# Splitting five of the seven half-wide products of the aggregates a second time (two-layer graph attention network, fp32)

## The chip, the cores and the metric

The kernel runs on one core of one Trainium2 chip. The metric is the device time of one execution in microseconds (us); a figure for a kernel is the median of several executions. The profile is one further execution, recorded by the hardware profiler.

## What is computed

Two layers of graph attention over N = 2708 rows of width D = 1024, all fp32. `adj` (2708 x 2708, int32) says which pairs of rows are joined.

```python
h = relu(layernorm(x))                      # layer 0
f, g = h @ Wf + bf, h @ Wg + bg
e = relu(f @ g.T)
a = softmax(where(adj > 0, e, -9e15), axis=1)
x = x + a @ (h @ W + bW)

h = relu(layernorm(x))                      # layer 1
hW = h @ W1
e = leaky_relu(hW @ a1 + (hW @ a2).T)
a = softmax(where(adj > 0, e, -9e15), axis=1)
x = x + relu(a @ hW)
```

Both kernels reorder this: `a @ (h @ W)` is taken as `(a @ h) @ W`, and `f @ g.T` as `h @ (Wf Wg^T) @ h.T` with the biases added as vectors. The score matrix is kept transposed: attended rows lie on partitions, attending rows in columns.

## The kernel before, in words

*Tiling.* The 2708 attending rows are cut into five column panels of 576, 576, 532, 512 and 512 (`width`). The attended rows are 20 tiles of 128, in ten pairs (`NQ` = 10), and a rest of 128 + 20 rows (`MONO` and `TINY`, the left-over tiles). The width of 1024 is two halves of `W` = 512, and each half four chunks of 128 (`NH` = 4).

*One level of Strassen.* Every large product is a 2 x 2 block product in the form that Winograd gave to Strassen's method: seven products of half-size blocks (`M1` to `M7`) in place of eight, with sums and differences of blocks before and after. In an aggregate the left blocks are halves of two paired row tiles, the right blocks the two halves, `lo` and `hi`, of a panel's columns. A half-wide product of panel p therefore streams h = `width[p]`/2 columns: 288, 288, 266, 256 and 256. Operations on the operands and the joins of the results run on VectorE (DVE in the profile); its additions and subtractions all have line L45, since a helper issues them.

*The stages of layer 0.* First M = Wf Wg^T. Then for each panel:

- `project_q` (L639) makes the right side of the scores, M times the panel's rows; in it `hT` (L643) holds the turned rows of the panel, in the two large buffers of pool `gts` that the aggregates' results `gT` use too.
- `scores` (L1115) goes through the ten pairs; each takes seven products of four matmuls (L1140) with the operands `As`, 512 KB a load, adds the biases, applies relu and the mask, and keeps the column maximum. Masks are made from `adj` a pair ahead.
- `softmax` subtracts the maximum, exponentiates on ScalarE and sums.
- `aggregate` (L841) multiplies the weights with the rows: `accumulate` (L603) takes the products in the order M1, M5, M2, M6, M3, M7, M4, each of 10 pairs x 4 chunks = 40 matmuls (L617) into four PSUM banks. The left operands `hc` are 512 KB loads of two pairs of one of seven prepared forms of the rows (`hg_d`, in DRAM). `left_over` (L877, matmuls on L883 and L887) adds the rest of 128 + 20 rows. `second` and `fourth` (L857, L864) make the differences of the weights that the later products need. `scale` (L931) divides by the sums on POOL.
- `project` (L965) multiplies the result with W, whose blocks `w` are loaded by `load_W` (L955), in matmuls of 512 columns (L1029); `finish0` (L1348) adds the residual and the bias and hands the finished rows to `rows_done` (L1283), which prepares layer 1: layernorm, the prepared forms of the rows (`pair_h`, L309), dot products and maxima.

Layer 1 has no scores matrix product. `weights1` (L1460) makes the weights from two vectors; then follow `aggregate` and `project` per panel.

*Order.* TensorE works through its list in program order. All loads are issued by SP in program order (L139), all stores by POOL (L143). Between the matmuls the helper `behind(rate)` (L198) works off a list of tasks, `later`, which `put` fills: each task may have a load that is issued a few tasks ahead. So the layernorm of later rows, the preparation of layer 1, the preparation of W (`prepare_W`, L1067) and the weights of layer 1 run beside the matmuls. Where `nc.hold` names VectorE, its program order is kept as well; elsewhere a scheduler orders it.

The main loop (L1423 to L1457) takes, for the first panels, `scores(p)`, `project_q(p+1)`, `aggregate(p)`, `project(p)`; after the first aggregate it empties the task list (`flush`, L1447). For the last two panels the projection comes a stage later: scores 4, projection 3, aggregate 4, projection 4.

*Buffers.* SBUF has 54 buffers of one panel row (`slots`, L118) for weights, sums and temporaries, and 12 of 4 KB per partition (`strm`, L119) through which everything streams that is loaded. PSUM has eight banks of 512 columns.

Of the kernel before, what the change touches and what calls it, by code (L numbers as in the profile page):

```python
# [57 lines left out]
def kernel(  # L58
# [59 lines left out]
    slots = ctx.enter_context(tc.tile_pool(name="slots", bufs=54))  # L118
    strm = ctx.enter_context(tc.tile_pool(name="strm", bufs=12))  # L119
# [34 lines left out]
    groups = [[q, q + 1] for q in range(0, NQ, 2)]  # L154
    group_of = {q: (i, j) for i, g in enumerate(groups) for j, q in enumerate(g)}
    assert sorted(group_of) == list(range(NQ))
    hg_d = [[dram.tile([P, 7, len(g), W], FP, name=f"hg{l}_d{i}") for i, g in enumerate(groups)] for l in range(2)]
    hsl_d = dram.tile([P, 2, NH, P], FP, name="hsl_d")
    hgl_d = [dram.tile([P, 2, W + P], FP, name=f"hgl{l}_d") for l in range(2)]
# [141 lines left out]
    def left_h(l, hm, ht):  # L301

        for e in range(2):
            store(hgl_d[l][:, e, :W], hm[e])
            for d in range(NH):
                g = slice(B32 * d, B32 * (d + 1))
                store(hgl_d[l][g, e, W:], ht[e][g, d * P:(d + 1) * P])

    def pair_h(l, q, ha, hb):  # L309
# [3 lines left out]
        if q >= NQ - F // 2:  # L313
            s1, s2, s3, s4 = (slot(f"g{i}")[:, :W] for i in range(4))
            i, j = group_of[q]
            for m, h in ((M1, ha[0]), (M2, hb[0]), (M4, hb[1])):
                store(hg_d[l][i][:n, m, j], h)
            on.tensor_tensor(s1, ha[1], hb[1], OP.add)
            on.tensor_tensor(s2, s1, ha[0], OP.subtract)
            for m, h in ((M5, s1), (M6, s2)):  # L320
                store(hg_d[l][i][:n, m, j], h)

            def rest():
                on.tensor_tensor(s4, hb[0], s2, OP.subtract)
                on.tensor_tensor(s3, ha[0], ha[1], OP.subtract)
                for m, h in ((M3, s4), (M7, s3)):
                    store(hg_d[l][i][:n, m, j], h)
# [7 lines left out]
        i, j = group_of[q]  # L335
        for m, h in ((M1, ha[0]), (M2, hb[0]), (M4, hb[1])):
            store(hg_d[l][i][:n, m, j], h)
        store(hg_d[l][i][:n, M5:M6 + 1, j], g1[:n])
        store(hg_d[l][i][:n, M7:M3 + 1, j], g2[:n])

    def rows_h(q, ha, hb):

        i, j = group_of[q]
        for m, h in ((M1, ha[0]), (M5, ha[1]), (M2, hb[0]), (M4, hb[1])):
            store(hg_d[0][i][:, m, j], h)
# [3 lines left out]
    def sums_h():  # L349

        def fetch(q, two):
            i, j = group_of[q]
            for m in (M1, M2):
                two.append(stream("hr", (P, 2, W)))
                load(two[-1], hg_d[0][i][:, m:m + 2, j])
# [6 lines left out]
        def second(q, two):  # L362
# [3 lines left out]
            i, j = group_of[q]  # L366
            store(hg_d[0][i][:, M6:M7 + 1, j], two[0])
            store(hg_d[0][i][:, M3, j], b0)
            store(hg_d[0][i][:, M5, j], b1)
            summed[0] += 1  # L370
        for q in range(NQ):
            two = []
            put(1.4, lambda q=q, two=two: first(q, two), lambda q=q, two=two: fetch(q, two))
            put(1.4, lambda q=q, two=two: second(q, two))

# [263 lines left out]
    def project_q(p, then={}):  # L639
# [3 lines left out]
        R = first_h if p == 0 else both("hT")  # L643
        lo, hi = (t.rearrange("p (c i) -> p c i", c=NH) for t in R)
        o = 0
        for t, n in pieces[p]:
            if p == 0:
                break
            for e, side in enumerate((lo, hi)):
                s = side[:, :, o:o + n]  # L650
                if t == TINY:
                    nc.scalar.copy(s, tinyT[:, e, :, :NY])
                elif t == MONO:
                    load(s, hsl_d[:, e, :, NM:])
                else:
                    q, k = pair_of[t]
                    load(s, hs_d[q][:, (BY_SCORES.index(M4 if k else M2) if e else 7 if k else BY_SCORES.index(M1))])
            o += n
        T1 = in_pairs("qT1")
        for g in range(2):  # L660
            sub(T1[g][:, :, :h], lo[:, 2 * g:2 * g + 2, h:w], lo[:, 2 * g:2 * g + 2, :h])
        sub(lo[:, :, h:w], hi[:, :, h:w], lo[:, :, h:w])

        def second():
            for g in range(2):
                sub(lo[:, 2 * g:2 * g + 2, :h], hi[:, 2 * g:2 * g + 2, h:w], T1[g][:, :, :h])

        def fourth():
            sub(hi[:, :, :h], hi[:, :, :h], lo[:, :, :h])
# [18 lines left out]
        def right(m, k):  # L688
            return {M1: lo[:, k, :h], M2: hi[:, k, :h], M3: hi[:, k, h:w], M5: T1[k // 2][:, k % 2, :h],
                    M6: lo[:, k, :h], M7: lo[:, k, h:w], M4: hi[:, k, :h]}[m]  # L690
# [150 lines left out]
    def aggregate(l, p, S, sm, then={}, rate=3.0):  # L841
# [28 lines left out]
        def left(m, q, d):  # L870
            i, j = group_of[q]
            if (m, i) not in hc:
                hc[m, i] = stream("hc", (P, 2, W))
# [706 lines left out]
```

## Time and profile before

| | us |
|---|---|
| median of 3 runs | 3132.52 |
| lowest and highest of them | 3129.16, 3133.04 |
| span of the profiled execution (the page gives no other time of it) | 3135.8 |
| PE (TensorE matmul) busy | 3053.1 |
| PEld (TensorE weight load) busy | 2266.1 |
| DVE (VectorE) busy | 1835.6 |
| ACT (ScalarE) busy | 450.3 |
| POOL (GpSimd) busy | 427.3 |

All times in the profile are microseconds of that one execution. SP issues the loads. An fp32 matmul appears as two records, each with its own weight load; a row of the profile writes the number of records as x80. The slices of the page cut the span into 40 equal parts, one digit each (9 is 90% or more). A view by stages cuts the span where TensorE's work changes, and gives the busy time of each engine in each stretch, the TensorE clock that was granted (PEclk), the mean busy share of the 16 DMA engines and what they moved. The chain of waits follows the work back from what ended last: each of its rows is a start, a duration, an engine, a tile and a line.

The whole kernel moves 666 MB through the DMA engines, 212 GB/s over the span. The aggregates of layer 0 for panels 1 to 4 take TensorE 148, 137, 132 and 132 us, those of layer 1 150, 138, 134 and 132 us.

### The profile page before, as it was taken

What the parts mean: (1) busy time and instruction counts of PE and PEld (TensorE: products, weight loads), DVE (VectorE), ACT (ScalarE), POOL (GpSimd) and SP (SyncE); (2) the same over time, 40 slices, a digit from 0 to 9 for tenths busy, and PEclk for the clock granted to TensorE, in tenths of its full rate; (3) what the DMA queues carried; (4) which work ended last, traced back from release to release, by engine and by line L of the source; (5) the groups of instructions that cost most, each with busy time, mean ns of one, the idle gap of its engine ahead of it and who ended that gap; (6) DMA issues with size and microseconds to landing.
All of it is one profiled execution on the core that took longest, in us unless ns stands there. A gap on an engine that the chain in (4) does not pass through costs nothing.

```text
span 3135.8 us, 36310 instructions
## 1 busy us (share of the span) xinstructions
PE 3053.1 (97%) x12694; PEld 2266.1 (72%) x12694; DVE 1835.6 (59%) x3767; ACT 450.3 (14%) x785; POOL 427.3 (14%) x654
## 2 busy tenths in 40 slices
PE   8998999899999999999999999998999999999998
PEld 4576777657877588886888885875757758678684
DVE  5766693776741686426973377758573571745612
ACT  3420020010200101101020002103131130311200
POOL 1421101310002110023000101021010020120202
PEclk9999999999999999999999999998999999999999
DMA  6989967988546796468955678597655565565655
GB/s 220 294 252 248 292 247 253 301 275 230 175 136 156 222 247 223 149 153 253 284 180 160 171 214 245 191 293 250 200 179 175 158 200 158 171 197 172 219 169 181
DMA packets 386278, 666.04 MB, mean 212 GB/s; under 512 B 171744, under 2 KB 212224, under 8 KB 386096
## 3 DMA queue, kind: packets, MB, share of 16 engines
q1 hardware_dynamic: 341936, 536.96, 56.9%
q0 software_dynamic: 44160, 126.76, 12.6%
q8 instruction: 101, 1.65, 0.2%
q14 instruction: 81, 0.66, 0.1%
HBM read 548.26 MB, written 115.30 MB: 212 GB/s over the span
## 4 chain that ended last, share of the span: by engine, by line
PE 81%; issue 6%; DVE 6%; DMA 5%; SPq 1%; POOL 1%; ACT 0%; POOLq 0%; DVEq 0%; ACTq 0%
PE gz L617 11%; PE gx L617 11%; PE gy L617 10%; PE sz L1140 6%; PE pz L1029 5%; PE gv L617 5%; PE sx L1140 4%; PE sy L1140 4%; PE px L1029 4%; PE py L1029 4%; PE M_ps L530 3%; PE qz L617 2%; PE qx L617 2%; PE qy L617 2%; DVE junk L45 1%
## 5 line engine op out<-in xcount | busy, mean ns | idle before, releaser
L1140 PE MATMUL sz<-B,As 128*128 128x288 f32 (+2 forms) x1200 | 295.9, 396 | 12.1 <-DVE st L45 7.9
L1140 PEld LDWEIGHTS sz<-B,As 128*128 128x128 f32 x1200 | 229.4, 192 | 63.1 <-DVE st L45 11.8
L933 POOL TENSOR_TENSOR gT<-gT,rr 128x2304 f32<-128x2304 f32 (+5 forms) x20 | 73.0, 3648 | 1081.4 <-DVE rr L45 979.3
L1140 PE MATMUL sx<-B,As 128*128 128x288 f32 (+2 forms) x800 | 201.5, 395 | 11.2 <-DMA As<-hs_d 9.1
L1140 PE MATMUL sy<-B,As 128*128 128x288 f32 (+2 forms) x800 | 199.3, 392 | 0.0
L617 PE MATMUL gz<-Sa,hc 128*128 128x288 f32 (+2 forms) x800 | 190.3, 399 | 5.9 <-DMA hc<-hg_d 5.9
L617 PE MATMUL gx<-P,hc 128*128 128x288 f32 (+2 forms) x800 | 187.0, 394 | 0.1
L617 PE MATMUL gz<-P,hc 128*128 128x288 f32 (+2 forms) x800 | 185.5, 392 | 0.0
L1140 PEld LDWEIGHTS sx<-B,As 128*128 128x128 f32 x800 | 152.5, 191 | 45.2 <-DMA As<-hs_d 10.1
L617 PE MATMUL gy<-T,hc 128*128 128x288 f32 (+2 forms) x800 | 184.2, 391 | 0.0
L617 PEld LDWEIGHTS gz<-Sa,hc 128*128 128x128 f32 x800 | 154.6, 194 | 40.0 <-DMA hc<-hg_d 6.4
L617 PEld LDWEIGHTS gx<-P,hc 128*128 128x128 f32 x800 | 152.4, 191 | 34.2 <-issue 3.7
L1140 PEld LDWEIGHTS sy<-B,As 128*128 128x128 f32 x800 | 152.3, 191 | 30.8
L617 PEld LDWEIGHTS gz<-P,hc 128*128 128x128 f32 x800 | 151.3, 190 | 31.6 <-issue 1.8
L617 PEld LDWEIGHTS gy<-T,hc 128*128 128x128 f32 x800 | 152.0, 190 | 30.5
L1029 PE MATMUL pz<-w,ps 128*128 128x512 f32 x320 | 142.1, 594 | 0.8 <-DVE pt L45 0.8
L1029 PE MATMUL py<-w,ps 128*128 128x512 f32 x320 | 141.9, 593 | 0.0
L1029 PE MATMUL px<-w,gT 128*128 128x512 f32 x320 | 141.0, 593 | 0.0
L143 POOL DMA_DIRECT2D out_dram<-x_res x180 | 89.2, 502 | 269.7 <-DVE x_res L45 264.5
L1029 PEld LDWEIGHTS pz<-w,ps 128*128 128x128 f32 x320 | 60.2, 190 | 77.1 <-issue 71.0
L1029 PEld LDWEIGHTS py<-w,ps 128*128 128x128 f32 x320 | 60.6, 190 | 75.5 <-issue 73.1
L530 PE MATMUL M_ps<-wgT,wfT 128*128 128x512 f32 x256 | 112.9, 597 | 1.6 <-ACT hsT L45 1.6
(319 smaller groups left out, 4894.9 us busy)
## 6 DMA issues: line engine op xcount, KB each, us to landing
hc<-hg_d SPq DMA_DIRECT2D x350, 512.0 KB, 3.7
As<-hs_d SPq DMA_DIRECT2D x150, 512.0 KB, 5.2
w<-wt_d SPq DMA_DIRECT2D x96, 512.0 KB, 4.9
w<-in_L_gnn_W_dram SPq DMA_DIRECT2D x72, 512.0 KB, 4.8
md<-md_d SPq DMA_DIRECT2D x56, 512.0 KB, 5.7
adj_i<-in_adj_dram SPq DMA_DIRECT2D x200, 128.0 KB, 5.2
hs_d<-hsT POOLq DMA_DIRECT2D x40, 512.0 KB, 7.2
As<-hs_d SPq DMA_DIRECT2D x50, 256.0 KB, 4.8
```

Source lines behind the costliest of these rows:

```text
L45: i = f(*a, **k)
L143: nc.gpsimd.dma_start(a, b)
L530: nc.tensor.matmul(ps, wfT[a][c // NH][:, c % NH, :], wgT[b][c], start=(c == 0), stop=(c == NC - 1))
L617: nc.tensor.matmul(ps[d], left(m, k, d), right(m, k), start=(start and k == 0), stop=(k == K - 1), skip_group_check=True)
L933: nc.gpsimd.tensor_tensor(of(e, s), of(e, s), by(s, k), OP.mult)
L1029: nc.tensor.matmul(ps, left[i][m][:, k, :], w_[k], start=(start and k == 0), stop=(k == NH - 1), skip_group_check=True)
L1140: nc.tensor.matmul(ps[:n, :h], lefts[q][:, i % 2, c, :n], B[m][c // 2][:, c % 2, :h], start=(start and c == 0), stop=(c == NH - 1), skip_g ...
```

## The change

**The aggregates of panels 1 to 4, in both layers, become `aggregate_quartered`.** `M1` and `M5` stay as before. The other five (`BY_QUARTERS`, in the order M2, M6, M7, M3, M4) are each split once more: a product of half-size blocks becomes seven products of quarter-size blocks. One such sub-product is five pairs of pairs (`NK` = 5) times two output chunks, ten matmuls with hb = h/2 columns (144, 133, 128, 128), and both output chunks share one PSUM bank.

```diff
+    def aggregate_quartered(l, p, S, sm, then={}, rate=3.0, fine=1.2):
...
+        def quarter_sums(m):
+            for k in range(NK):
+                r11, r12, r21, r22 = (part_of(m, k, i) for i in ((0, 0), (0, 1), (1, 0), (1, 1)))
+                four = slot("quarter", (P, 4, WX // 4))
+                t = {n: four[:, i, :hb] for i, n in enumerate((M5, M6, M7, M4))}
+                sub(t[M5], r12, r11)
+                sub(t[M6], r22, t[M5])
+                sub(t[M7], r22, r12)
+                sub(t[M4], r21, t[M6])
+                sums[m, k] = t
...
+        def product(m, n, ps, start):
+            quarters_until(l, m)
+            t = stream("hc2", (P, NK, WH))
+            if n in (M1, M2, M4):
+                load(t, hr_d[l][:, m, int(n == M4), int(n != M1)])
+            else:
+                load(t, hs2_d[l][:, m, {M5: 0, M6: 1, M7: 2, M3: 3}[n]])
+            for k in range(NK):
+                for d in range(2):
+                    nc.tensor.matmul(ps[:, d], t[:, k, d * P:(d + 1) * P], inner_right(m, n, k),
+                                     start=(start and k == 0 and d == 0), stop=(k == NK - 1), skip_group_check=True)
+            behind(fine)
...
+        before_next = {M2: lambda: (fourth(), quarter_sums(M6)), M6: lambda: quarter_sums(M7),
+                       M7: lambda: quarter_sums(M3), M3: lambda: quarter_sums(M4)}
+        left_out = None
+        for m in BY_QUARTERS:
+            V = in_pairs("V")
...
+            X = bank2("gx")
+            product(m, M1, X, True)
+            nc.scalar.copy(c21, X)
+            if left_out:
+                left_out()
+            Z = bank2("gz")
+            product(m, M6, Z, True)
+            add(c12, Z, c21)
+            Y = bank2("gy")
+            product(m, M5, Y, True)
+            add(c22, Y, c21)
+            if m == M7:
+                corner()
+            if m in before_next:
+                before_next[m]()
+            product(m, M2, X, False)
+            if m not in more_of:
+                nc.scalar.copy(c11, X)
+            product(m, M7, Z, False)
+            add(c22, Z, c22)
+            product(m, M3, Y, False)
+            if m in more_of:
+                U = bank2("gu")
+                left_over({(0, 0): X, (0, 1): Y, (1, 0): Z, (1, 1): U}, *more_of[m], [(1, 1)])
+                nc.scalar.copy(c11, X)
+            add(c12, Y, c12)
+            if m in more_of:
+                add(c22, U, c22)
+            into_place(m, V, 0)
+            def left_out(m=m, V=V, Z=Z, c21=c21):
+                product(m, M4, Z, False)
+                add(c21, Z, c21)
+                into_place(m, V, 1)
...
```

`product` of the last sub-product, M4, follows after the first of the next product (`left_out`). `second` (20 subtractions) and `quarter_sums(M2)` follow in M5; `fourth` writes into the tiles of M5. `scale` stays on POOL. The left-over rows go in by twice as many matmuls of half the columns; the tiny rows in DRAM are stored as two chunks side by side for that (`hgl_d`, W + 128 columns before, W + 256 after).

**The rows' quarter sums.** The seven forms of the rows are stored by quarters (`hr_d`, in place of `hg_d`), and for each of the five products four sums of quarters are made once a layer and stored (`hs2_d`): 25 tasks a layer.

```diff
+    def put_quarters(l, m, k):
+        two = []
+        def fetch():
+            two.append(stream("hq", (P, 4, WH)))
+            load(two[0], hr_d[l][:, m, :, :, k].rearrange("p h f c -> p (h f) c"))
+        def go():
+            a11, a12, a21, a22 = (two[0][:, i] for i in range(4))
+            o = stream("hq2", (P, 4, WH))
+            s1, s2, s3, s4 = (o[:, i] for i in range(4))
+            add(s1, a21, a22)
+            sub(s2, s1, a11)
+            sub(s3, a11, a21)
+            sub(s4, a12, s2)
+            store(hs2_d[l][:, m, :, k], o)
+            made_quarters[l, m] = made_quarters.get((l, m), 0) + 1
+        put(1.7, go, fetch)
+    def quarters_until(l, m):
+        while made_quarters.get((l, m), 0) < NK:
+            one()
```

The 25 tasks of layer 0 are put after the first aggregate, those of layer 1 by `rows_done` when a group of pairs is complete (`quads_met`).

**Order and buffers.** The main loop takes each projection after the next panel's scores; the empty-the-list call after the first aggregate is replaced by `flush_W`, which works off the list after the scores of panel 1 only until W is prepared (`todo_W` counts that).

```diff
-    slots = ctx.enter_context(tc.tile_pool(name="slots", bufs=54))
-    strm = ctx.enter_context(tc.tile_pool(name="strm", bufs=12))
+    slots = ctx.enter_context(tc.tile_pool(name="slots", bufs=53))
+    strm = ctx.enter_context(tc.tile_pool(name="strm", bufs=10))
...
         if p == 0:
...
+            B = project_q(1, hooks)
+            ahead[0] = 1
+            G[0] = aggregate(0, 0, S, got["sm"], {M4: lambda: sums_until(NQ), M5: prepare_W, **masks})
+            ahead[0] = 2
+            for m in BY_QUARTERS:
+                for k in range(NK):
+                    put_quarters(0, m, k)
+            continue
+        if p == 1:
+            flush_W()
+            spread_wa()
+        nc.hold = ("vector",)
+        project(0, p - 1, G.pop(p - 1), finish0(p - 1), hooks)
+        nc.hold = ()
+        if p == NP - 1:
+            scores_before()
+        G[p] = aggregate_quartered(0, p, S, got["sm"])
         if p + 1 < NP:
-            B = project_q(p + 1, hooks)
...
-            flush()
...
+            B = project_q(p + 1, masks)
...
-            then = {M3: lambda p=p: take_shifts(p + 1), M7: lambda p=p: take_weights(p + 1)}
-        g = aggregate(1, p, S, sm, then, rate=4.0)
+            then = dict(zip((M7, M3) if p else (M3, M7), (lambda p=p: take_shifts(p + 1), lambda p=p: take_weights(p + 1))))
+        g = (aggregate_quartered if p else aggregate)(1, p, S, sm, then, rate=4.0)
```

In `project_q`, `hT` no longer uses the two large buffers but four of `strm` (`stream("hT", (P, 2, WX))`), loaded and subtracted in halves of two chunks.

## The prediction

> **What bounds the kernel now.** I read first the busy shares and slices of the page, then the stages (busy time of each engine in stretches cut where the TensorE work changes), then the chain of waits inside one aggregate, then single instructions.
>
> ```profile
> PE 3053.1 (97%) x12694; PEld 2266.1 (72%) x12694; DVE 1835.6 (59%) x3767; ACT 450.3 (14%) x785; POOL 427.3 (14%) x654
> PE   8998999899999999999999999998999999999998
> ```
>
> TensorE is busy in every slice. Of the chain of waits, this is the whole aggregate of layer 0, panel 3:
>
> ```profile
> 1646.00 17.27 PE gx L617 x80
> 1663.27 17.27 PE gy L617 x80
> ...
> 1738.33 10.36 PE gz L617 x48
> 1748.69 1.73 PE gw L883 x8
> 1750.42 0.64 PE gw L887 x8
> 1751.06 7.10 PE gz L617 x32
> ```
>
> No wait is in it. A half-wide product is 80 records, two per fp32 matmul: 40 matmuls, 17.27 us, 0.2159 us a record at 256 columns. Panel 1 (288 columns) shows 19.40 us for the same 80, panel 2 (266) 17.93. So a record takes 0.0028 us + 0.8324 ns per column, and TensorE time is columns streamed. The stages:
>
> ```profile
> core 0: us, PE busy (x) PEld busy (x) DVE busy (x) ACT busy (x) POOL busy (x), PEclk, DMA share, GB/s
> 667.00:819.00 152.00, 149.38 (x629) 114.81 (x628) 105.03 (x228) 3.99 (x7) 12.17 (x21) 0.99 0.81 235
> 1219.00:1269.00 50.00, 50.00 (x237) 43.83 (x237) 43.07 (x80) 17.38 (x30) 0.14 (x1) 1.00 0.41 137
> 2090.00:2157.00 67.00, 54.02 (x135) 24.80 (x133) 48.37 (x121) 10.47 (x18) 12.84 (x23) 0.90 0.99 362
> 540.00:580.00 40.00, 34.08 (x129) 25.95 (x128) 28.82 (x80) 0.00 (x0) 10.31 (x20) 0.91 1.02 408
> ```
>
> These are the scores of panel 1, the right side for panel 3, the last projection of layer 0, and 40 us inside the first aggregate. The reader is to see: VectorE at 86% (43.07 of 50) costs TensorE nothing; where the DMA share reaches 1.0, TensorE loses time (34.08 of 40); and the scores already hold the DMA engines to 0.81.
>
> [...] after an idle stretch two loads of 0.19 us each span 0.30, so the second starts 0.11 after the first.
>
> ```profile
> 2104.99 0.30 PEld L1029 LDWEIGHTS pz<-w,ps 128*128 128x128 f32 x2 [1.61 <-DVE pt L45]
> 2105.53 0.19 PEld L1029 LDWEIGHTS pz<-w,ps 128*128 128x128 f32 x1 [0.24 <-issue]
> ```
>
> [...] packed instructions start about 0.08 us before the record ahead ends:
>
> ```profile
> 1240.64 0.42 DVE L45 TENSOR_TENSOR m<-qy,m 128x256 f32<-128x256 f32 x1
> 1240.98 0.70 DVE L45 TENSOR_TENSOR sm<-sm,Sa 128x532 f32<-128x532 f32 x1
> 1241.60 0.42 DVE L45 TENSOR_TENSOR m<-qy,m 128x256 f32<-128x256 f32 x1
> ```
>
> [...]
>
> **The change part by part.** *Products.* Five products of each of eight aggregates become seven products of half depth, half rows and half columns: 7 x 10 matmuls, 140 records, in place of 80. At 144 columns a record is 0.1227 us by the line above, at 133 0.1135, at 128 0.1093. Per product 19.40 becomes 17.18, 17.93 becomes 15.89, 17.27 becomes 15.30. Times five: 11.1, 10.2, 9.9, 9.9 for panels 1 to 4, 41.1 a layer, 82.2 in all. The left-over tiles stream the same columns in twice the records, +0.02 us for each of 16 plus the twenty-row rest, about 1 in all. **-81**, all on the path, since the path is TensorE.
>
> *Weights.* A record of 128 columns (0.109) now meets a load of 0.11. [...] I take 1.5 ns on the 700 records of each of four panels (3 and 4, both layers), 4, and see no excess at 133 and 144: **+4**.
>
> *Quarters of the rows.* 25 tasks per layer load 0.52 MB, make four sums and store 0.52 MB. For layer 0 the changed program's SP order puts four of these loads between the score loads of each of the first six tile pairs of panel 1. Such a pair takes TensorE seven products of eight records, 56 x 0.2425 = 13.6 us. It moves score operands 1.84 MB, adjacency 0.58, mask 0.29 and now four times 1.05: 6.9 MB. At 362 GB/s, what 67 us sustained at a share of 0.99, that is 19.1 us; at 408, 16.9; at 290 (235 over the share 0.81), 23.8. So 5.5 us too much for 6.25 pairs, 34, less about 7 that loads ahead of need cover: **+27**, bounds 14 and 57. SP issues in order, so the score loads stand behind the quarter loads and TensorE waits for them. VectorE has there about 10 us a pair (105 over ten) + 16 additions of 0.34 = 15.4 against 13.6: busy, but below the 19.1.
>
> *Quarters of the weights, partial results.* Each quartered aggregate adds 100 subtractions at 128 to 144 columns (0.21 packed: 21 us), and about 10 more of evictions and joins. In the VectorE order of the changed program the four aggregates of layer 0 hold 289, 311, 330 and 301 instructions, since the row work of the panel before now falls there. Packed they take 102, 107, 115 and 108 us. TensorE's stages of before, 148, 137, 132 and 132 us, become 137, 127, 122 and 122: 74, 84, 94 and 89%. A sub-product (20 records, 2.2 us at 128) draws 0.655 MB, 300 GB/s. With ten loads of 0.52, five quarter tasks of 1.05, 3.7 of row stores and some 5 of masks and other loads an aggregate moves about 42 MB, 344 GB/s at the narrow panels, under 362. I take nothing for panel 1, 4, 7 and 4 for the others: **+15**, bounds 0 and 60.
>
> *Layer 1.* VectorE holds 70 to 84 us of 122 to 139. At the end of M5 it has, in one run, 20 quarter sums (4.2), 20 subtractions of `second` (6.8), eight of `fourth` (2.7) and four evictions (1.4), 15 us from the middle of M5 on; M5's second half (8.6) and the first four sub-products (8.7), which need no free bank of it, cover 17. After the last exponentials nearly nothing is left: 2 each, **+8**, bounds 0 and 24.
>
> *Moves.* Projections go behind the next scores with their weight loads, x loads and bias DMAs, SP's and POOL's alike; TensorE's count is unchanged, and scores, at 0.74 to 0.91 of the DMA engines, are relieved of the row work. The forced emptying of the task list after the first aggregate goes; what is late next is the same preparation before panel 0's projection, one stage later. `hT` moves into the streaming pool, which shrinks from 12 to 10 buffers: four are held for 50 us at 137 GB/s, with six left for two loads per product of 7 us. 0; if that cover fails, a load of 5 us per product, 35 a stage. The waits of before (8.3 at the last column maximum, 8.1 and 5.9 on loads) stay.
>
> Sum: -81 + 4 + 27 + 15 + 8 = -27 on the profiled execution, whose span of 3135.8 us stands 3.3 above the median of 3132.5. 3135.8 - 27 - 3.3 = 3105.5; I say 3105.
>
> **The rivals.** *All hidden:* loads and VectorE keep up as in every aggregate of before; only the +4 and some 8 remain: 3135.8 - 81 + 12 - 3 = 3064. For it: a chain without a wait. Against it: the arithmetic of 19.1 against 13.6. *The DMA engines decide in layer 0 (slower):* if the mixture holds only 290 GB/s, the aggregates' 42 MB take 145 us: +8, +18, +23, +23, and the scores +57; with 12 for the rest -81 + 72 + 57 + 12 = +60, 3192. At 320 (aggregates 131 us, +22; scores 21.6 a pair, +43) nothing is left of the gain: that is the point from which it decides. For it: 235 at 0.81. Against: 362 and 408 with larger packets. *Weights set the pace (slower):* [...] It decides from 0.123 us per record at 128 columns (17.27/140). Against: loads 0.11 apart. *It doesn't save what it says:* TensorE's order shows the 140 records, so only the waits can.
>
> **How the numbers follow.** A measurement tells 0.2% (6 us) from no change. Forecast (3080 to 3126) 0.45; all hidden (below 3080) 0.22; losses eat the gain (3126 to 3139) 0.10; DMA decides 0.18; weights 0.05. Faster 0.67, same 0.10, slower 0.23. The range 3058 to 3150 leaves out the weights, the worse two thirds of the DMA case and a sliver of the hidden one: 0.2.
>
> **What would show it.** 128-column records 0.109 to 0.111 us apart; about 137 us for the aggregate of panel 1 of layer 0, 122 to 135 for the others; the scores of panel 1 near 180 us with waits of the score matmuls on `As` and a DMA share near 1; quartered aggregates of layer 0 with short waits on `hc2` or on V's additions. I am wrong if records stand 0.12 us or more apart, if the scores of panel 1 keep 152 us, or if layer 0's aggregates are longer than before.

## The result, and the profile after

The changed kernel takes 3223.4 us, the median of 4 runs (3220.0 to 3226.0); before, beside it, 3132.8. The ratio is 1.028, with a 95% interval of 1.0265 to 1.0299. I had said 3105 and faster. The profiled execution has a span of 3218.2 us against 3135.8, so 82.4 us have to be found.

The first lines of the page after:

```profile
PE 3014.6 (94%) x15606; PEld 2338.5 (73%) x15606; DVE 2184.8 (68%) x4956; ACT 478.5 (15%) x871; POOL 487.3 (15%) x704
...
PE   8998989866999999999999999996999999999998
```

TensorE's work fell: 3053.1 to 3014.6 us busy, although the busy time also counts records at a low granted clock (in one place below, eight of 288 columns take 4.21 us, and 2.10 a little later). Slices 9 and 10 are a new hole, and slice 28 went from 8 to 6. The stages, cut at the first matmul of each in both traces, in us:

| stages | before | after | difference |
|---|---|---|---|
| up to the end of the scores of panel 0 | 383.5 | 381.5 | -2.0 |
| right side for panel 1 | 63.8 | 79.3 | +15.5 |
| first aggregate of layer 0 (plain in both) | 167.5 | 172.7 | +5.2 |
| scores of panel 1, projection 0 | 200.0 | 282.5 | +82.5 |
| aggregates of panels 1 to 4, layer 0 | 148.1, 137.0, 132.0, 132.1 | 138.2, 133.9, 134.2, 128.5 | -14.4 |
| right sides for panels 2 to 4 | 150.5 | 154.8 | +4.3 |
| scores of panels 2 to 4, projections 1 to 3 | 571.5 | 563.6 | -7.9 |
| projection 4 (last of layer 0), with the maxima | 67.0 | 89.6 | +22.6 |
| first aggregate of layer 1 (plain in both) | 151.7 | 161.3 | +9.6 |
| aggregates of panels 1 to 4, layer 1 | 150.2, 138.4, 133.3, 132.0 | 142.4, 129.5, 126.7, 124.1 | -31.2 |
| the rest | | | -1.8 |

Single stages in the view by stages, with the columns of the stages shown before. First the scores of panel 1 in the changed kernel:

```profile
638.00:870.00 232.00, 168.56 (x636) 125.49 (x637) 131.31 (x297) 0.81 (x2) 34.34 (x44) 0.85 0.83 251
```

Then layer 0's aggregate of panel 3, before the change and after:

```profile
1646.00:1778.00 132.00, 132.00 (x629) 114.16 (x629) 35.83 (x82) 4.24 (x10) 7.56 (x3) 1.00 0.58 159
```

```profile
1679.00:1813.00 134.00, 126.00 (x993) 119.43 (x991) 116.03 (x322) 18.87 (x37) 28.37 (x36) 1.00 0.89 310
```

Last, in the changed kernel, the last projection of layer 0 and layer 1's aggregate of panel 3:

```profile
2173.60:2254.00 80.40, 54.24 (x115) 22.88 (x115) 46.54 (x97) 9.79 (x16) 19.31 (x27) 0.85 0.99 325
...
2859.00:2986.00 127.00, 125.89 (x1006) 120.30 (x1005) 91.47 (x243) 22.59 (x45) 11.91 (x11) 1.00 0.83 269
```

In layer 1 the splitting works: TensorE is busy 125.9 of 127 us, and the four quartered aggregates have DMA shares of 0.75 to 0.86. In layer 0, at shares of 0.86 to 0.89, it works less well: the aggregate of panel 3 keeps TensorE busy for 126.0 of 134 us and is longer than before. The chain of waits in the last aggregate of layer 1 shows what a record costs now:

```profile
3119.51 2.23 PE gx L1039 x20
3121.75 4.47 PE gz L1039 x40
```

Forty records of 128 columns take 4.47 us, 0.1117 apart, where the line of the kernel before gave 0.1093. At 133 and 144 columns they stand 0.1133 and 0.1225 apart, as it gave.

**The hole at slices 9 and 10.** TensorE's longest wait in the scores of panel 1 (total, times, longest), before the change and after, then two of SP's after:

```profile
PE sz L1140 <- DVE st L45: 2.0, 1, 2.0
```

```profile
PE sx L1365 <- DMA As<-hs_d: 60.7, 8, 12.1
```

```profile
SPq L139 <- PE sz L1365: 41.6, 14, 5.5
SPq L139 <- DMA hs_d<-hq: 36.9, 8, 5.8
```

The profile leaves trailing numbers out of names: `hs_d<-hq` is the store of a quarter task into `hs2_d`, and further down `hc` also stands for `hc2`. SP waits for `sz` when a load needs a buffer that TensorE still reads, and for that store when an earlier task still holds the buffer. Before, TensorE waited for no score load, and the stage was 151.9 us long. Now it waits for them eight times in ten tile pairs. SP's own list shows one such turn, and TensorE's the end of it:

```profile
719.45 0.32 SPq L139 DMA_DIRECT2D As<-hs_d  x1
721.39 6.17 SPq L139 DMA_DIRECT2D hq<-hr_d  x2
727.64 3.22 SPq L139 DMA_DIRECT2D adj_i<-in_adj_dram  x4
730.91 3.61 SPq L139 DMA_DIRECT2D adj_t<-in_adj_dram  x4
734.62 1.26 SPq L139 DMA_DIRECT2D As<-hs_d  x2
```

```profile
740.59 4.21 PE L1365 MATMUL sx<-B,As 128*128 128x288 f32 x8 [11.48 <-DMA As<-hs_d]
744.59 4.09 PE L1365 MATMUL sz<-B,As 128*128 128x288 f32 x16
748.52 2.10 PE L1365 MATMUL sy<-B,As 128*128 128x288 f32 x8
```

Two quarter loads (`hq`) hold SP for 6.17 us, since the buffer that they are to fill is still held; the eight adjacency loads come after them, and the score load `As` after those. TensorE waits 11.48 us, and then its first eight records take 4.21 us, where eight later ones take 2.10. From 740.0 to 744.8 us the granted clock was 0.51, from there to 760.0 it was 1.00; over the stage it is 0.85, for 0.99 before. All eight waits for score loads show it: after the seven of 4.3 to 12.1 us the first eight records take 3.6 to 4.2 us, after the one of 0.5 us 2.2. The waits, 61 us, and the growth of TensorE's busy time in the stage, 19 (149.4 to 168.6), of which the slower records behind these waits are about 16, make up 80 of the 81 us by which the stage grew.

### The profile page after: what moved, and what is told of

The parts are those of the page before. It is cut to its first block, busy times and chain, and to the rows that moved or that the text cites. A ratio compares the mean times of both kernels' runs of the same rounds, so it can differ in the third digit from the quotient of the medians.

```text
span 3218.2 us, 43997 instructions
## 1 busy us (share of the span) xinstructions
PE 3014.6 (94%) x15606; PEld 2338.5 (73%) x15606; DVE 2184.8 (68%) x4956; ACT 478.5 (15%) x871; POOL 487.3 (15%) x704
## 3 DMA queue, kind: packets, MB, share of 16 engines
q0 software_dynamic: 51360, 153.24, 14.8%
## 4 chain that ended last, share of the span: by engine, by line
PE 63%; issue 16%; DMA 11%; DVE 5%; SPq 3%; POOL 2%; ACT 0%; POOLq 0%; DVEq 0%; ACTq 0%
PE sz L1365 7%; PE sx L1365 5%; PE gz L1039 5%; PE sy L1365 4%; PE pz L1246 4%; PE gy L646 4%; PE gx L646 4%; PE px L1246 3%; PE gy L1039 3%; PE gx L1039 3%; PE py L1246 3%; PE M_ps L559 3%; PE qz L646 3%; SPq L139 3%; PE qy L646 2%
## 5 line engine op out<-in xcount | busy, mean ns | idle before, releaser
L1039 PE MATMUL gz<-quarter,hc 128*128 128x128 f32 (+2 forms) x2400 | 292.2, 279 | 6.7 <-DMA hc<-hs_d 4.5
L1039 PEld LDWEIGHTS gz<-quarter,hc 128*128 128x128 f32 x2400 | 282.4, 191 | 9.5 <-issue 5.0
L1365 PE MATMUL sx<-B,As 128*128 128x288 f32 (+2 forms) x800 | 214.5, 414 | 68.0 <-DMA As<-hs_d 63.6
L143 POOL DMA_DIRECT2D mk_d<-mask x55 | 36.1, 656 | 698.7 <-DVE mask L45 690.7
L1089 POOL TENSOR_TENSOR gT<-gT,rr 128x1024 f32<-128x1024 f32 (+5 forms) x16 | 61.0, 3813 | 531.7 <-DVE gT L45 531.7
L45 ACT COPY V<-gx 128x256 f32<-128x256 f32 (+2 forms) x80 | 30.4, 380 | 677.5 <-PE gx L1039 363.7
L45 DVE TENSOR_TENSOR V<-gz,V 128x256 f32<-128x256 f32 (+2 forms) x120 | 51.8, 432 | 115.3 <-PE gz L1039 115.1
L1246 PEld LDWEIGHTS px<-w,gT 128*128 128x128 f32 x320 | 60.8, 193 | 82.7 <-issue 81.2
```

What stands on the lines that cost most here:

```text
L45: i = f(*a, **k)
L143: nc.gpsimd.dma_start(a, b)
L1039: nc.tensor.matmul(ps[:, d], t[:, k, d * P:(d + 1) * P], inner_right(m, n, k), start=(start and k == 0 and d == 0), stop=(k == NK - 1), sk ...
L1089: nc.gpsimd.tensor_tensor(t, t, by(s, NH, k), OP.mult)
L1246: nc.tensor.matmul(ps, left[i][m][:, k, :], w_[k], start=(start and k == 0), stop=(k == NH - 1), skip_group_check=True)
L1365: nc.tensor.matmul(ps[:n, :h], lefts[q][:, i % 2, c, :n], B[m][c // 2][:, c % 2, :h], start=(start and c == 0), stop=(c == NH - 1), skip_g ...
```

## The experiments

Times are medians beside runs of the kernel before (3131 to 3137 us); stages are of each run's profiled execution. The code shows the lines that matter; "..." stands for others. "The changed kernel" is the starting point where nothing else is said.

**1. The quarter sums in place.**

```diff
-            o = stream("hq2", (P, 4, WH))
-            s1, s2, s3, s4 = (o[:, i] for i in range(4))
-            add(s1, a21, a22)
-            sub(s2, s1, a11)
-            sub(s3, a11, a21)
-            sub(s4, a12, s2)
-            store(hs2_d[l][:, m, :, k], o)
+            add(a22, a21, a22)
+            sub(a21, a11, a21)
+            sub(a11, a22, a11)
+            sub(a12, a12, a11)
+            store(hs2_d[l][:, m, :, k], two[0])
...
```

> The row quarter sums are made in place, so that a task takes one streaming buffer and not two; loads, stores, bytes and additions stay as they are. Theory (buffers): in the scores of panel 1 SP stands 6.2 to 6.5 us per tile pair on a quarter load that waits for a buffer held by an earlier quarter store, and the adjacency and score loads stand behind it. With half of the buffers turned over, the scores of panel 1 fall from 231 us to between 180 and 205, the whole by 25 to 50 us. Rival 1 (the DMA engines' throughput: 6.9 MB a pair at the 255 GB/s of that stage is 27 us): the bytes are the same, so 231 stays within 5. Rival 2 (VectorE, whose additions stand between the masks): the additions are the same, so 231 stays within 5.

3190.8 us, ratio 1.019 (1.0161 to 1.0217). The scores of panel 1 fall from 233.0 to 206.0 us with the same bytes and the same additions: buffers are part of it, though a smaller one than I expected (180 to 205). The two rivals, by which the stage would have stayed as long, don't hold as the only cause. TensorE's wait for the score loads is now:

```profile
PE sx L1363 <- DMA As<-hs_d: 33.1, 7, 7.5
```

It has about halved and has not gone. The first aggregate of layer 1 goes from 161.3 to 152.7 us: most of what the tasks worked off there cost it goes away with the second buffer.

**2. Quarter loads issued by another engine.**

```diff
-            load(two[0], hr_d[l][:, m, :, :, k].rearrange("p h f c -> p (h f) c"))
+            (load if l else nc.scalar.dma_start)(two[0], hr_d[l][:, m, :, :, k].rearrange("p h f c -> p (h f) c"))
```

> In layer 0 the quarter loads are issued by ScalarE, which has 0.4 us of work in the scores of panel 1, in place of SP. Theory (SP's order): a quarter load that waits for a buffer no longer holds up the adjacency and score loads; the scores of panel 1 fall from 231 us to between 160 and 185, the whole by 45 to 70 us. If it is buffers and not order (the quarter loads take the buffers that score loads need, whoever issues them): a fall of less than 25 us. Rival 1 (DMA throughput) and rival 2 (VectorE): no change within 5 us.

3221.1 us, ratio 1.029 (1.0271 to 1.0315): nothing gained. The scores of panel 1 take 233.6 us, and TensorE's wait for the score loads is 60.9. The place of the quarter loads in SP's list is not what makes the stage long; now SP's `As` loads themselves wait for the buffers (two runs of four of them hold SP for 11.5 and 12.4 us). All tiles of the streaming pool share ten buffers, whoever issues the load.

**3. Layer 1 alone quartered.**

```diff
-            for m in BY_QUARTERS:
-                for k in range(NK):
-                    put_quarters(0, m, k)
...
-        G[p] = aggregate_quartered(0, p, S, got["sm"])
+        G[p] = aggregate(0, p, S, got["sm"])
```

> Layer 0 keeps the plain aggregates and has no quarter tasks; order, buffers and layer 1 are those of the changed kernel. All theories: the scores of panel 1 take 150 to 155 us again (before: 152) and layer 0's aggregates 148, 137, 132 and 132; so 3223 - 79 + 14 = about 3158 us. If the new order and the smaller streaming pool are part of the trouble in those scores, they stay above 165 us.

3132.2 us, ratio 1.000 (0.999 to 1.0011), 26 us below what I expected: besides the scores of panel 1 (151.1 us, as all theories had it), the last projection falls from 89.6 to 73.3 us and the right sides for panels 2 to 4 by 8. Layer 0's quartering costs time there too.

**4. Only the new order.** All aggregates plain, no quarter tasks.

> All aggregates plain: only the new order of the stages, hT in the streaming pool and the pools of 53 and 10 are left of the change. My prediction took these at 0. By the two traces they cost 15 us in the right side for panel 1, 5 in the first aggregate, 13 in the last projection of layer 0 and 19 in the first aggregate of layer 1, and give 10 back in the scores of panels 2 and 3: 3133 + 43 = about 3176 us. If the 13 and 19 come from the quartered aggregate's buffers and not from the order: about 3145.

3191.4 us, above both of my figures. Layer 1 took 165, 152, 146 and 132 us: I had left the exchanged hooks of layer 1 in, and a plain aggregate takes M3 ahead of M7, so that from panel 2 on the weights are called for ahead of the shifts that belong to them. Only layer 0 is read from this run: right side for panel 1 79.7, scores of panel 1 151.1, last projection 72.2.

**5. Only the new order, hooks in the old place.**

```diff
...
-            then = dict(zip((M7, M3) if p else (M3, M7), (lambda p=p: take_shifts(p + 1), lambda p=p: take_weights(p + 1))))
+            then = dict(zip((M3, M7), (lambda p=p: take_shifts(p + 1), lambda p=p: take_weights(p + 1))))
```

> The run with only the new order, with layer 1's hooks in the old place (shifts of the next panel at M3, its weights at M7), which suit the order of the products of a plain aggregate. Layer 1's aggregates go back to 150, 138, 133 and 132 us, where the run with the hooks exchanged had 165, 152, 146 and 132. The whole: 3191 - 48 = about 3143 us, that is +12 for the new order, hT's buffers and the pools, which my prediction took at 0. If layer 1 stays long, the smaller pools do it and not the hooks.

3150.0 us, ratio 1.0057 (1.0034 to 1.0079). Layer 1 is back at 150.2, 138.4, 133.3 and 132.0, so the hooks had done it. I had expected 3143. New order and pools alone cost 16 us (11 to 25 by the interval), where I had taken 0: 15.0 in the right side for panel 1 and 6.4 in the last projection, against 10 gained in the scores of panels 2 and 3.

**6. Buffers of their own for layer 0's quarter tasks** (two of the pool of 53 each), with sums in place.

```diff
-            two.append(stream("hq", (P, 4, WH)))
+            two.extend(slot("hq", (P, 2, WH)) for _ in range(2)) if l == 0 else two.append(stream("hq", (P, 4, WH)))
...
```

> As the run with the sums in place, but in layer 0 the quarter tasks take two buffers each of the pool of 53 and none of the streaming pool; bytes and additions stay, loads and stores are two of 256 KB for one of 512 KB. Theory (shared streaming buffers): the score and adjacency loads no longer wait for a buffer that a quarter store holds; the scores of panel 1 fall from 231 us (206 in place) to between 155 and 180, the whole to about 3145 to 3170. Rival (DMA throughput, the rest of what in place did not give back): 62 MB at no more than 290 GB/s are over 213 us, so the stage stays at 200 or more.

3178.6 us, ratio 1.016 (1.014 to 1.0175). The scores of panel 1 take 197.0 us: 9 less than in place, far from the 155 to 180 of my theory and close to the rival. In the middle of that stage, this run and then the changed kernel:

```profile
640.00:780.00 140.00, 109.25 (x404) 80.91 (x403) 101.42 (x234) 0.00 (x0) 39.88 (x57) 0.90 1.04 318
```

```profile
640.00:780.00 140.00, 88.70 (x307) 65.48 (x306) 78.93 (x183) 0.41 (x1) 20.36 (x25) 0.80 0.82 250
```

The last two columns are DMA share and GB/s: with shared buffers the DMA engines were busy 0.82 of the time, with buffers of their own they are full. So buffers hid a second limit. Share times duration says how large it is. Without quarter tasks, in the new order (experiment 5), the stage of 151 us is this:

```profile
640.00:790.00 150.00, 149.48 (x638) 115.79 (x637) 95.92 (x196) 0.80 (x2) 13.70 (x19) 0.99 0.79 212
```

That is 0.79 x 151 = 119 us of all sixteen engines (before the change it was 0.81 x 152 = 123, with row work that the new order takes elsewhere). The changed kernel has 0.83 x 233 = 193, experiment 1 0.92 x 206 = 190, experiment 2 0.81 x 234 = 190, and this run 0.97 x 197 = 191: the same 58 MB need about 190 us of the engines, however long the stage. The 25 tasks add some 74 us to 119 in a stage of 151, which by this estimate can't be much shorter than 190 with them. The estimate rests on the shares; no run takes bytes alone out of this stage.

**7. The same, spread evenly, hT of panel 1 in the large buffers.** The second rate is that at which tasks are worked off beside the scores of panel 1.

```diff
...
-        rates = (0.6, 1.0, 0.65, 0.65, 0.65)
+        rates = (0.6, 0.55, 0.65, 0.65, 0.65)
```

> Both layers quartered; quarter sums in place, those of layer 0 in buffers of their own; hT of panel 1 in the large buffers; and in the scores of panel 1 the task rate 0.55 for 1.0, which puts about 2.4 quarter loads between the score loads of each of the ten pairs where there were four in six of them. Theory (with own buffers, 197 us, the DMA engines set that stage: share 1.0 from 640 to 780 us at about 315 GB/s): the same 55 MB, spread, need 174 us; 172 to 182 for the stage, the whole 3179 - 22 - 20 = about 3137. Rival (something else holds the score loads, VectorE or SP's order): the stage stays at 190 or more.

3163.1 us, 26 above what I expected. The scores of panel 1 take 176.3 us, inside the range, but projection 0 after them 65.6 for 49.4: together 241.9 us against 246.4 without the spreading. The last two tasks moved on into that projection, where the DMA share rose from 0.75 to 0.89. But TensorE's longest wait there is one for VectorE:

```profile
PE sp_ps L245 <- DVE mcol L45: 9.6, 1, 9.6
```

VectorE works in program order there and reaches `mcol` only after it has waited 10.5 us for a quarter load, which stands in SP's list behind 32 loads of `x` rows (22.8 us). What was won in one stage was lost to the order of loads in the next.

**8. hT of panel 1 in the large buffers, layer 0 plain, layer 1 quartered with sums in place.**

```diff
...
-        lo, hi = ((halved(t) for t in first_h) if p == 0 else
+        lo, hi = ((halved(t) for t in (both("hT") if p else first_h)) if p < 2 else
...
```

> Layer 0 plain as in the run with only layer 1 quartered (3132 us), its quarter sums in place, and hT of panel 1 back in the two large buffers. Theory: the 16 us more in the right side for panel 1 come from hT's four streaming buffers, for which the md loads wait: 80 us go back to 64. In place, the first aggregate of layer 1 loses its wait on hc (161 to 152). Together about 3132 - 16 - 8 = 3108 us. Rival (the order put the loads of h's sums behind hT's in SP's list whatever buffer they go to): the right side stays near 80, and the whole above 3118.

3095.0 us, ratio 0.989 (0.9874 to 0.9914): faster than both kernels. The right side for panel 1 takes 57.4 us, where I expected 64; the first aggregate of layer 1 151.6. In the changed kernel TensorE waited in that right side:

```profile
PE sp_ps L245 <- DVE mcol L45: 8.7, 1, 8.7
PE qx L646 <- DMA md<-md_d: 6.5, 1, 6.5
PE qy L646 <- DMA md<-md_d: 4.1, 2, 3.6
```

None of these three waits is left in this run. The loads `md` were late because hT held four of the ten streaming buffers while the sums of h (`hr`) held others: SP waited 30.2 us there for their stores. VectorE, which the first wait is put down to, had itself waited 15.7 us for `hr` loads.

**9. The old order with layer 1 quartered**, sums in place, hT in the large buffers.

> The order of the stages of the kernel before, hT in the large buffers for all panels, layer 0 plain, layer 1 quartered with sums in place. Theory: nothing of layer 0 is later than before but for the 25 quarter tasks of layer 1 in it; layer 1 keeps its 31 us: 3132 - 31 + about 5 = 3106 us. If the quarter tasks cost more in the old order, where the projections with row work stand next to the aggregates' loads: 3120 or more.

3170.2 us, ratio 1.013 (1.0114 to 1.0145); I had expected 3106. Layer 1 keeps its gain, but the scores of panels 1, 2 and 3 take 170.5, 166.9 and 149.0 us for 151.9, 138.7 and 137.7 before the change. In the old order the quarter tasks of layer 1 fall into these scores, five in each, where the DMA share before was 0.81 to 0.91; in the new one into the aggregates, where it was 0.55 to 0.7. But it is not engine time that ran out: the share in this run's three stages is 0.81, 0.84 and 0.93. SP waits in them 19.3, 18.2 and 17.0 us for buffers that stores of the row work hold (7.1, 2.5 and 14.0 before), and this run has ten streaming buffers where the kernel before has twelve. With these pools and tasks the old order is 75 us slower than the new (experiment 8), which I had taken to cost and bring nothing; which part of the 75 the tasks have, and which the smaller pool, is not separated.

**10 and 11. What holds layer 0's quartered aggregates?** The weights' quarter sums left out (`inner_right` always returns a quarter), and loads of two blocks of five, used in turn:

```diff
-            t = stream("hc2", (P, NK, WH))
+            t = stream("hc2", (P, 2, WH))
...
-                    nc.tensor.matmul(ps[:, d], t[:, k, d * P:(d + 1) * P], inner_right(m, n, k),
+                    nc.tensor.matmul(ps[:, d], t[:, k % 2, d * P:(d + 1) * P], inner_right(m, n, k),
```

> The changed kernel with the 100 subtractions a quartered aggregate for the quarter sums of the weights left out: the sub-products read quarters themselves, so the output is not the reference's. Theory A (VectorE, 104 to 116 us of 134 busy in the aggregates of panels 2 and 3 of layer 0, sets the loss there): they fall from 133.9 and 134.2 us to about 126 and 122, and the short waits on V in layer 1 go (142.4 to 140, 129.5 to 127.5). Theory B (DMA at a share of 0.88 sets it): within 2 us of 133.9 and 134.2.

> The changed kernel, in which each load of a sub-product's rows brings two of the five blocks (256 KB for 640), used in turn, so that the output is not the reference's. Buffers, number of loads, VectorE and TensorE stay. The aggregates of layer 0 move about 26 MB in place of 40. Theory B (DMA at a share of 0.86 to 0.89 sets their loss): the aggregates of panels 2, 3 and 4 of layer 0 fall from 133.9, 134.2 and 128.5 us to about 127, 123 and 123; layer 1 stays within 2. Theory A (VectorE sets it; leaving out 100 subtractions took only 2.8 us from one of the three): they stay within 3 us.

Without the sums 3217.3 us, ratio 1.028; the aggregates of panels 2 to 4 take 134.4, 131.4 and 130.1 us. With fewer bytes 3206.6 us, ratio 1.024; 132.6, 127.8 and 130.8, and 80.1 for the last projection. Neither theory holds for all: panel 3 gets 2.8 us from the sums left out and 6.4 from the bytes left out, panel 2 next to nothing from either, panel 4 nothing, and panel 1 is even longer in both (141.4 and 144.3 us for 138.2). In other runs with the unchanged quartered aggregate panel 3 takes 133.0 to 138.3 us, so the 131.4 without the sums lies only 1.6 below the lowest of them. What holds these aggregates is not settled. Layer 1 stays within 1.2 us in both: its short waits on V (VectorE's partial results) are not made by these sums.

**12. Layer 0 quartered without its row tasks**; its sub-products read quarters of the stored rows in place of their sums.

> Both layers quartered, hT of panel 1 in the large buffers, layer 1's sums in place; but layer 0 has no tasks for its row quarter sums: its sub-products read the stored rows' quarters in place of the sums, so the output is not the reference's. Loads and matmuls of the aggregates stay. Against the run with layer 0 plain (3095 us): theory, the quartered aggregates of layer 0 give 15 us (10, 3, -2, 4) and cost 8 in the right sides and 16 in the last projection, so that they don't pay even with free sums: 3095 + 9 = about 3104 us. Rival (those costs come from the tasks too, those of layer 1 that are worked off there): 3080 us or less.

3119.7 us, ratio 0.995 (0.9929 to 0.9967), 25 above layer 0 plain (experiment 8), where I had expected 9. The four aggregates take 145.2, 134.5, 137.0 and 128.7 us: 3.8 less than plain in all, while the last projection takes 14.8 more and the right sides 10.2 more. In this kernel layer 0's splitting would not pay even if the sums of its rows were free.

**13 to 17. The last projection of layer 0.** What SP issues at the end of the aggregate before it, before the change and after:

```profile
2049.98 0.32 SPq L139 DMA_DIRECT2D hc<-hg_d  x1
2054.29 3.84 SPq L139 DMA_DIRECT2D w<-in_L_gnn_W_dram  x2
...
2064.59 4.48 SPq L139 DMA_DIRECT2D x_res<-in_x_dram  x8
...
2086.39 0.96 SPq L139 DMA_DIRECT2D w<-in_L_gnn_W_dram  x2
```

```profile
2157.47 0.36 SPq L139 DMA_DIRECT2D hc<-hr_d  x1
2157.93 9.53 SPq L139 DMA_DIRECT2D maskl<-mk_d  x13
2167.51 0.94 SPq L139 DMA_DIRECT2D w<-in_L_gnn_W_dram  x2
```

Before, the aggregate ended at 2090.3 and its last load went out 40 us earlier; after, 2173.6 and 16 us earlier. Its loads now last 2.2 us each in TensorE, so ten buffers hold at most 22 us of work, where twelve held 41 of 3.45 each. All that stands behind them in SP's list (masks 9.5 us, x rows 24) starts later. Five runs are on that. 13 issues the third product's weights first:

```diff
-        ws = {m: load_W(l, m) for m in order[:2]}
+        ws = {m: load_W(l, m) for m in order[:3 if by_pair and l == 0 else 2]}
```

> The changed kernel, in which the last projection of layer 0 issues the weights of its third product ahead of its x rows. Theory (in the handover the x rows wait for buffers that the quartered aggregate holds, and the weights stand behind them in SP's order): TensorE's waits of 11 and 6 us on w go, and the stage from the last projection to the first aggregate of layer 1 falls from 89.6 to about 75 us; the whole to about 3208. Rival (the x rows themselves are late, and the evictions with them): the same wait comes back on the banks, 85 us or more.

3224.3 us; 89.8 us for the stage. The wait came back at the next product's weights (9.5 us on `wt_d`), which the rival did not name either. 14 and 15 put the x rows into streaming buffers (they are loaded into the pool of 53, as the masks are, so not everything that is loaded streams through `strm`), in the changed kernel and in the best version:

```diff
-                xs[t] = row_halves("x_res", t == MONO)
+                xs[t] = row_halves("x_res", t == MONO or p == NP - 1)
```

> The changed kernel with the x rows of the last projection of layer 0 in four streaming buffers, not in eight of the pool of 53. Theory (the quartered aggregate holds the pool of 53 to its end, the x rows wait for it, the weights stand behind them): SP issues them before the aggregate ends and the last projection falls from 89.6 us to about 75, the whole to about 3208. Rival (streaming buffers are as short there, since weights and masks use them): 85 or more.

> Layer 0 plain, layer 1 quartered with sums in place, hT of panel 1 in the large buffers (3095 us), and the x rows of the last projection in streaming buffers: that projection 73 us to about 68, the whole 3088 to 3093. If streaming buffers are short there: 3095 to 3105.

3228.3 and 3105.5 us; the stage takes 94.5 and 78.2 us, 5 more in both. My theory, that the pool of 53 makes the x rows late, is wrong. 16 and 17 issue the x rows inside the aggregate:

```diff
+        early = {}
+        if p == NP - 1:
+            last_finish = finish0(p)
+            early[M7] = lambda: last_finish[0](list(full(NP - 1)))
-        G[p] = aggregate_quartered(0, p, S, got["sm"])
+        G[p] = aggregate_quartered(0, p, S, got["sm"], early)
...
```

> The changed kernel, in which the x rows (with their masks and bias) of the last projection of layer 0 are issued in the aggregate before it, after its fourth product (M7), two products ahead of its end. Theory (their place in SP's list behind the aggregate's last loads makes them, and the weights behind them, late): the last projection falls from 89.6 us to between 68 and 75, the aggregate of panel 4 from 128.5 to at most 133, the whole from 3223 to about 3208. Rival (the DMA engines at a share of 0.99 hold that stage, whatever the order): 85 us or more.

> Layer 0 plain, layer 1 quartered with sums in place, hT of panel 1 in the large buffers (3095 us), and the x rows of the last projection issued after the product M3 of the aggregate before it: 73 us to between 62 and 68, the whole 3084 to 3091. By the rival: 3093 or more.

3226.3 and 3114.6 us. The projection falls to 72.4 and 66.1 us, as the theory had it, but the aggregate, for which the theory allowed 133 us, grows from 128.5 to 152.4 and from 132.1 to 152.9. Its wait in the first of the two:

```profile
PE gx L1039 <- DMA hc<-hr_d: 19.9, 2, 19.6
```

There SP issues the 32 x rows from 2127.5 to 2147.1 us and the next load `hc2` only then; TensorE goes on at 2153.6. So the wait follows the place of the x rows in SP's list, 17 to 24 us of it, and these two moves shift it without removing it. A lead of up to 34 us (ten loads of 3.45, in the plain aggregate of the last run) didn't cover it either; masks stand between the loads there as well. What part the DMA engines have is not separated: from 2130 to 2175 us of the first of the two runs their share is 0.91 to 1.03.

## Why the prediction was wrong

*What bounds the kernel, and the products.* Right. By the columns of its records the TensorE stream fell by about 81 us, and layer 1 shows most of the gain.

*Weights, +4.* Right in kind: 2.4 ns more per record at 128 columns in place of 1.5, 6.7 us on 2,800 records. The 1.5 was my estimate. A row of before could have checked it: where rows are turned (`h_ps`, L399), eight records of 128 columns, each with a weight load, stand 0.109 apart.

*Quarters of the rows, +27 with bounds 14 and 57: the step that failed.* It was +81: 54 of the 109 us between -27 and +82. Two terms were wrong. First, "At 362 GB/s" priced a mixture at the rate of a stage without adjacency loads. The same view held a better price, share times duration: 0.81 x 152 = 123 us already taken, and 25 tasks of 1.05 MB at 362 GB/s add 73, together 196 in a stage of 152, +44. The runs gave 193, and 45 is what was left with buffers of their own (197.0 against 151.9). Second, "SP issues in order, so the score loads stand behind the quarter loads" named the wrong resource: issuing them elsewhere changed nothing. Ten buffers in turn carry score, adjacency and quarter tiles; a task took two and gave one back only when its store had landed, 36 us in all (27 by sums in place, 9 by buffers of their own). The sign that I had named, a DMA share near 1, did not come: it was 0.83, since the buffers kept the engines from filling. I had counted transfers and additions, and not for how long each task holds what.

*Aggregates of layer 0, +15 with bounds 0 and 60.* They kept 14.4 of the 41 us that the products save; with the 4 for weights and left-over tiles set aside that is +23. I had 0 for panel 1, 4, 7 and 4, and it was about 0, 6, 11 and 5: the order of the panels is right, the size two thirds, and panel 3 at 134.2 us for 132.0 is one of the signs of being wrong that I had named. The 0.21 us of a packed subtraction, an estimate from wider ones (0.42 us at 256 columns, 0.70 at 532, less 0.08 of overlap), held: at 128 columns they start 0.20 apart and last 0.27. Even the 14.4 is not firm: in experiments 1, 6, 7 and 12, where the scores of panel 1 are shorter, panel 1's aggregate takes 143 to 145 us and the four keep only 4 to 8.

*Layer 1, +8.* Right: 31.2 of 41.1 gained, 10 lost, with its share of the weights in it. What I left out is the first aggregate of layer 1, which is plain and paid 9.6 us for the tasks worked off in it, nearly all through their second buffer (in place it takes 152.7 for 151.7).

*Moves, 0.* Wrong. "four are held for 50 us at 137 GB/s, with six left" is the cover that failed: 15.5 us for panel 1, where the sums of h use the pool at the same time (my fallback was 35 a stage; panels 2 to 4 lost 4 in all). I moved the projections with their x loads and did not ask how far ahead SP runs once the loads are used up in 2.2 us each: 22.6 us in the last projection, of which 6 come with plain aggregates too (experiments 3, 5 and 8). And I gave the new order no gain, though it takes the row work out of the scores: 10 us in the scores of panels 2 and 3.

*The rivals.* "The DMA engines decide in layer 0" had the right side and half the mechanism, and 290 GB/s with +57 in those scores was nearer than my own 362 (58 MB in 193 us are 300 GB/s); its aggregates at 145 us did not come. At 0.18 it was too low, and its bound at 57 left no room for buffers. "Weights set the pace" is excluded: 0.1117, with the turning point at 0.123; how far beyond it the records could lie, no trace of before showed.

*The version that beats both* is experiment 8, 3095.0 us, 1.1% below the kernel before: the splitting where it is cheap (layer 1), the new order, sums in place, and one buffer choice undone. It has 30 from layer 1, 10 from the scores, 6 from the right side for panel 1 (57.4 us for 63.8), and pays 6 in the last projection.

## What to carry to other kernels

Price an added transfer in engine time, not bytes: the DMA share of the stage times its length is what is already spent, and what is added must fit into the rest (by this estimate, in the scores of panel 1 119 of 151 us were spent and 74 came on top; the stage took 197 with buffers of their own). Then count buffers: which tiles take turns in a pool, who frees each, and how many microseconds of work the pool holds once each tile is used up faster. The finer products here saved TensorE 81 us by their columns, and shortened the lead of everything that stands behind their loads: ten buffers held at most 22 us of work, where twelve had held 41.

## What the runs showed that I had not expected

A pool shared by several kinds of tiles couples loads across issuing engines: with the quarter loads on ScalarE the stage stayed at 233.6 us, 0.6 from the 233.0 with SP. By share times duration, quarter tasks of 1.05 MB cost (193 - 119)/25 = 3.0 us of all sixteen DMA engines each, 355 GB/s, while the stage's own 32 MB took 119 us, 269 GB/s. And in long rows of 128-column records 0.1117 us apart, each with a weight load (these start 0.112 apart), TensorE lost only 2.4 ns per record.
